# The last graph's final stage in quarters, with three forget products on ScalarE, its stores on SyncE, and a new plan order

## Chip, cores and metric

The kernel runs on one core of a Trainium2 chip. The metric is the device time of one execution in microseconds (us); the median of three runs is compared. A profile of one execution stands beside them: it covers the span from the first to the last instruction, and a little over 3 us of the execution's own time lie outside it.

The engines of a core are named as the profile does: PE is TensorE (matrix products; PEld its weight loads), DVE is VectorE, ACT is ScalarE, POOL is GpSimd, SP is SyncE, which here only issues transfers. Each engine runs its own instructions strictly in order. A transfer is issued by an engine's queue ("SPq", "ACTq") and an instruction that waits holds everything behind it on its engine.

## What is computed

Sixteen graphs of 1024 nodes with 128 features pass through four layers; `adj` is a dense 1024 x 1024 matrix per graph. Each layer adds its result to x. The pieces that matter here are layers 2 and 3.

```python
# layers 0 and 1: three cosine convolutions; then adj aggregation and an MLP
x = x + adapt_conv3(relu(layernorm(x)), adj, ...)
x = x + mlp((1 + eps) * h + h^T adj)            # h = relu(layernorm(x))

# layer 2 (attention)
h = hn @ W                                        # hn = relu(layernorm(x))
attn = softmax(where(adj > 0, tanh(s1[:, None] + s2[None, :]), -1e15))
x = x + where(sum(adj, axis=1) == 0, hn, attn @ h)

# layer 3 (gated attention); x below is relu(layernorm(x))
h = x @ W_w.T + W_b
e = (h @ A) @ h.T;  e = e + e.T
att = softmax(where(adj > 0, e, 0), axis=1) * adj
hp = relu(att @ h)
i, f, o = sigmoid of three linear maps of concat(x, hp)
out = x_in + o * tanh(sigmoid(i * hp + f * x))
```

The last two lines are the final stage: `i`, `f` and `o` are one number per node each (the input, forget and output gates).

## The kernel before

**Tiling.** A graph's 1024 nodes are 8 blocks of 128 (NB = 8); a row buffer `[128, 8*128]` holds all nodes with the nodes of a block on the partitions. Products with the 1024 x 1024 matrices are cut in 8 source blocks and two halves of 512 columns, or, by nodes, in 8 x 8 pieces of 128 columns (`accumulate`, L1543, and `accumulate_nodes`, L1554).

**Order by a plan.** The function `tile_adj_preln` does not emit instructions as it goes. Every step is recorded by `op` (L1071) with its engine, the buffers that it reads and writes and a function that emits it. A step gets a rank: `batch * PERIOD + TIMES[key][nth]`, where the key is made of the layer, the engine and the buffer's name, with own lists for the first two and the last two graphs (" <0", " <1", " >1", " >0"). `Plan.order()` (L136) then picks, again and again, the ready step with the lowest rank whose new buffers fit into the limits of KINDS (L332: how many buffers of a kind there may be in all, and for graphs behind the oldest). The list that results is emitted in that one order, so it fixes the order on every engine and every queue. Steps of up to two later graphs (AHEAD = 2) are mixed in between.

**Layer 2 of a graph** (`layer2`, L1781): `psP` (PE), copies to h (ACT L1813), the products p1 (PE L1867) for s1, then for each of 8 source blocks tanh (ACT L1878), exp (ACT L1882), times the adjacency (DVE L1886), and the sum acc2 (PE L1554). At the end `rden`, `o`, `alone` and x (DVE L1899 to L1907, L1295).

**Layer normalization** (`layernorm`, L1311): statistics on DVE (L1321 to L1332), the power on POOL (L1173), then the scaling half on DVE (L1349), half on ACT (L1356).

**Layer 3** (`layer3`, L1913): sq (PE L1422, and L1439 which adds transposed pieces copied by ACT L1480), a mask of adj (DVE L1956), the masked e and its peak (DVE L1978 and L1987), exp (ACT L1998), times adj (DVE L2007 in two halves; in graph 14, for the odd blocks, POOL L2003), the reciprocal of the sum (DVE L2012), hs (ACT L2016), the sum acc3 (PE L1543); then hpT (ACT L1273), its transposition psN (PE L1251) and the copy hp (ACT L2057).

**The final stage** is the inner function `finish(lo, hi)` (from L2066), for the blocks lo to hi:

1. gate = three columns of hp plus three of h (DVE L2084), tanh (ACT L2108), times 0.5 plus 0.5 (DVE L2109): the three gates.
2. z = hn * forget gate: per block on DVE (L2114) for the last graph, one step on POOL (L2120) otherwise.
3. z = hp * input gate + z: per block on DVE (L2102), or two steps on POOL (L2095, L2096) for graph 14.
4. two tanh on ACT (L2088, L2089): the sigmoid, and the tanh of it.
5. z = z * output gate + x: as step 3.
6. the store of z, issued on ACT's queue (L2127).

For the last graph `finish` runs twice, for blocks 0 to 3 and 4 to 7 (HALVES); for the others once for all eight.

On SyncE's queue, in a middle graph, stand the loads of adj (L1588, and L1630, four issues for each of 8 blocks of adjT), x (L1571), and the store and reload of the transposed pieces (by_hbm L1524, got L1534; near_hbm L1502, back L1512), among others.

Of the kernel before, what the change touches and what calls it, by code (L numbers as in the profile page):

```python
# [12 lines left out]
ALU = mybir.AluOpType  # L13
# [201 lines left out]
def tile_adj_preln(  # L215
# [40 lines left out]
    FLAGS = set("CabcdkxhyzTGmrHWMD3nA")  # L256
# [62 lines left out]
    for load_it in first:  # L319
# [13 lines left out]
        "adjT": ("big", 16, 16), "adjL": ("big", 13, 5), "x": ("big", 5, 3), "w4": ("big", 23, 33),  # L333
        "chunk": ("big", 11, 11), "near": ("near", 2, 1), "quart": ("big", 6, 6), "back": ("big", 7, 1),
        "got": ("got", 1, 1), "ps": ("bank", 8, 8), "acc": ("bank", 7, 4), "small": ("small", 28, 22),
        "row": ("row", 4, 5), "hbm": ("hbm", 2, 3), "hrow": ("hrow", 2, 2), "mask": ("mask", 5, 5),
        "dot": ("dot", 7, 7),
# [4 lines left out]
        "T DMA raw <0": [-13.9, -43.4, -13.95, -48.95, -53.5, -67.75, 2.25, -52.65],  # L342
        "T PE raw <0": [-11.75, -9.15, -8.55, -9.1, -8.85, -11.75, -15.15, -5.25, -12.95, -2.15, 5.8, -17.1,
            -12.75, -12.8, 23.5, 34.25],
        "T ACT adjT <0": [-39.35, -14.15, -18.8, -16.75, -18.35, -7.35, -20.95, -34.55, -13.9, 3.5, 10.4,
            11.05, 16.4, 6.55, -0.6, 4.55],
        "T DVE su <0": [76.75],
        "x DMA x <0": [-13.95, -80.5],
        "0 DVE st <0": [-43.9, -15.15],
        "0 DVE mv <0": [-13.35],  # L350
        "0 POOL rstd <0": [-26.4],
        "0 DVE nb <0": [-22.3],
        "0 DVE hn <0": [-22.25],
        "0 ACT hn <0": [-27.2],
        "0 PE ps <0": [-11.4, -10.65],
        "0 ACT hT <0": [-67.75, -79.6],
        "00 PE psP <0": [-8.6, -54.95],
        "00 DVE h <0": [-22.8, -12.8],
        "00 PE ps <0": [-15, -14.15],
        "00 ACT hTn <0": [-14.35, -18.05],  # L360
        "00 ACT sq <0": [-18.7, -18.25],
        "00 DVE ss <0": [-11.3, -25.55, -15.65],
        "00 POOL rn <0": [-19.1],
        "00 PE sq <0": [-14.45, -7.15, -13.2, -16.05, -11.25, -11.2, -3.15, -2.9, -10.85, 0.7, -11.3, 9.3,
            -12.6, -11.7, 23.5, 14.15, -11.4, -12.7, 28.4, -31.65, 19.7, 36.7],
        "00 ACT near <0": [-18.15, -50.8, -13.85, 12.5, 7.6, 30.05],
        "00 DVE ew <0": [-9.05, -39.7, -6.9, -14.8, -2, 4.75, 8.6, 8.65, 5.75, 2.8, 8.75, -1.6, 7.15, 23.85,
            8.65, 14.9],
        "00 ACT quart <0": [-34.4, -12.1, -34.4, 2.65],
        "00 PE acc0 <0": [-0.8, 4.75, 21.5, 10.9, 1.35, 11.05, 26.05, 32.2, 25.7, 26.55, 27.25, 32.3, 24.45,  # L370
            37.95, 28.35, 29.65],
        "00 POOL params <0": [7.2, 10.25, -5.45, 41.9, 25.85, 20.85, 19.55],
        "00 DMA params <0": [-59.3],
        "00 DVE params <0": [40.65, 44.5, 44.1, 85.55, 81.35],
        "00 PE params <0": [41.95, 46.35, 76.45],
        "00 ACT hT <0": [47.25, 49.1],
        "01 PE psP <0": [-8.35, -10],
        "01 DVE h <0": [48.25, 48.85],
        "01 PE ps <0": [50.4, 52.7],
        "01 ACT hTn <0": [48.4, 52],  # L380
        "01 ACT sq <0": [25.85, 23.6],
        "01 DVE ss <0": [53.65, 33.25, 45.65],
        "01 POOL rn <0": [58.05],
        "01 PE sq <0": [39.9, 53.85, 55, 62.45, 57.8, 58.8, 57.7, 55.5, 49.4, 55.2, 47.35, 62.6, 62, 70.1,
            70.9, 59.9, 70.35, 65.3, 73.9, 62.25, 71.8, 75.4],
        "01 ACT near <0": [40.7, 64.95, 54.05, 64.2, 64.55, 76.4],
        "01 DVE ew <0": [54.65, 71.95, 59.1, 63.15, 60.75, 57.45, 60.35, 72.35, 62, 67.3, 67.6, 74.35, 63.35,
            68.2, 70, 75.65],
        "01 ACT quart <0": [27.55, 57.25, 60, 62.2],
        "01 PE acc0 <0": [63.6, 54.45, 58.6, 75.3, 64.9, 70.85, 62.65, 68.65, 59.35, 55.85, 71.9, 77.45,  # L390
            75.15, 78.85, 55.75, 76.95],
        "01 ACT hT <0": [75.95, 78.9],
        "02 PE psP <0": [56.85, 79.65],
        "02 DVE h <0": [75.4, 75.95],
        "02 PE ps <0": [77.25, 82.75],
        "02 ACT hTn <0": [79.4, 85.7],
        "02 ACT sq <0": [82.15, 71.35],
        "02 DVE ss <0": [76.25, 83.5, 84.75],
        "02 POOL rn <0": [93.55],
        "02 PE sq <0": [88.1, 87.8, 87.1, 91.65, 86.4, 90.15, 90.5, 90.25, 90, 94.25, 93.25, 96.75, 86.65,  # L400
            72.2, 90.25, 102.65, 102.75, 91.2, 103.25, 107.25, 94.75, 105.75],
        "02 ACT near <0": [77.55, 111.75, 89.25, 88.25, 64.25, 97.7],
        "02 DVE ew <0": [87.55, 88.4, 88.7, 84.4, 100.55, 95.75, 101.5, 84.8, 100.9, 106.1, 101.25, 106.65,
            86.6, 98.5, 89.25, 96.95],
        "02 ACT quart <0": [87.7, 88.8, 92.6, 97.3],
        "02 PE acc0 <0": [88.1, 96.95, 93.4, 96.95, 96.8, 99.1, 105.6, 89.8, 105.15, 107.3, 109.7, 110.7,
            106.1, 107.25, 100.3, 112.3],
        "02 DVE x <0": [95.3, 119.3],
        "T DMA adjT <1": [-196.95, -203.05, -216.2, -199.3, -194.4, -213.7, -216.25, -222.2],
        "T DVE adjT <1": [-137.45, -132.6, -132.15, -120.3, -114.25, -114.7, -109.45, -109.25],  # L410
        "T ACT su <1": [-112.25, -101.7, -91.85, -99.6, -96.95, -98.45, -73.5, -89.85],
        "1 DVE st <0": [115.9, 117],
        "1 DVE mv <0": [104.1],
        "1 POOL rstd <0": [113.1],
        "1 DVE nb <0": [120.95],
        "1 DVE hn <0": [113.7],
        "1 ACT hn <0": [134.9, 123.1],
        "1 DVE x <0": [142.15, 140.4, 142],
        "1 DMA adjL <0": [73.65, 69.65, 70.5, 72.6, 137.9, 140.25, 103.9, 109.9],
        "1 DVE adjL <0": [117.85, 77.2, 117.9, 112.65, 124.45, 128.5, 136.25, 134.45],  # L420
        "1 PE acc1 <0": [116.85, 125.15, 129.35, 131.55, 130.25, 139.9, 127.9, 129.3, 129.15, 130.2, 133.75,
            126.35, 132.45, 137.05, 135.2, 135.8],
        "1 ACT g <0": [126.85, 131],
        "1 PE py <0": [137.25, 137.2, 141.6, 137.5],
        "1 ACT y1 <0": [139.75, 138.3, 143.15, 139.8],
        "1 PE py2 <0": [137.75, 128.75],
        "2 DVE st <0": [142.85, 134.25],
        "2 DVE mv <0": [124.2],
        "2 POOL rstd <0": [144.35],
        "2 DVE nb <0": [145.05],  # L430
        "2 DVE hn <0": [147.9],
        "2 ACT hn <0": [129.45, 155.45],
        "2 PE ps <0": [149.7, 146.8],
        "2 ACT hnT <0": [139.55, 69.3],
        "2 DVE alone <0": [138.4],
        "2 DVE x <0": [161.8, 184.9, 184.95],
        "2 PE psP <0": [157.25, 149.45, 149.4],
        "2 ACT h <0": [143.95, 126.95, 127],
        "2 DVE hrow <0": [152.75],
        "2 PE pf <0": [162.6],  # L440
        "2 ACT hfl <0": [164.9],
        "2 PE pt <0": [161.2],
        "2 ACT sr <0": [161.25],
        "2 DMA sd <0": [165.2],
        "2 DMA s1 <0": [163.65],
        "2 DVE h <0": [162.4],
        "2 ACT e2 <0": [144.05, 141.25, 144.1, 150.85, 151.5, 172.6, 151.55, 172.65, 172.65, 172.55, 172.7,
            169.7, 175.8, 179.7, 173.4, 171.75],
        "2 DVE e2 <0": [129.85, 111.65, 158.25, 168.4, 91.05, 87.6, 83.25, 88.25, 170.45, 170.4, 171.75,
            173.1, 164.2, 164.1, 179.1, 179.1],  # L450
        "2 PE acc2 <0": [166.95, 171.9, 153, 177.75, 168.15, 153.4, 178.1, 177.75, 164.45, 167.35, 177.75,
            177.75, 153.2, 172.45, 166.3, 183.1, 171.45, 178.3, 180.65, 182.95, 180.95, 177.55, 175.7, 157.2],
        "2 DVE rden <0": [191.25, 127.75, 127.75, 191.6],
        "3 DVE st <0": [189.2, 171.65],
        "3 DVE mv <0": [191.5],
        "3 POOL rstd <0": [193.55],
        "3 DVE nb <0": [154.25],
        "3 DVE hn <0": [161.35],
        "3 ACT hn <0": [188.7, 253.8],
        "3 PE ps <0": [203.7, 195.9, 200.55, 165.7],  # L460
        "3 ACT hnT <0": [191.15, 186.3],
        "3 PE pg <0": [204.35, 201.8],
        "3 ACT gT <0": [198.15, 200.95],
# [683 lines left out]
    def blk(b, lo, hi, w=D):  # L1147

        return (b, lo * w, hi * w)
# [1099 lines left out]
```

## Time and profile before

| | us |
|---|---|
| median of 3 runs (lowest, highest) | 2362.98 (2362.1, 2363.3) |
| the profiled execution | 2363.82 |
| its span | 2360.7 |
| mean granted TensorE clock | 0.997 of full speed |

| engine | busy us | share of the span |
|---|---|---|
| VectorE | 2069.4 | 88% |
| ScalarE | 1427.9 | 60% |
| GpSimd | 251.6 | 11% |

TensorE's work is the same for every graph, but the first graph starts with nothing to overlap and the last ends with nothing to overlap: the shares above are means over three unlike stretches. How they differ is read from the busy time by windows, from the chain of waits (the work that ended last, followed back from the end) and from the timeline.

The rows of the final stage, in order of time: hp copies of the last graph end at 2348.80; the two gate steps on VectorE start at 2348.50 and 2348.84 (0.17 each), the two gate tanhs at 2348.86 (0.40 together); the forget products at 2349.31 and 2351.23 (four each, 0.88 and 0.87); the products with hp at 2350.18 and 2352.01 (four each, 1.14); the first half's tanh pair at 2351.35, the second's at 2354.71; the last product ends at 2357.26, its store is issued at 2357.35 and the span ends at 2360.7.

Durations that recur below, from the groups of the same page and from the single lines: L1998 exp of 128x1024 1.14 us, L2007 (128x512) 0.67, L1956 (mask, 128x1024) 0.69, L1978 (128x512) 0.68, L2016 (128x128 on ScalarE) 0.40, L1356 (128x128 on ScalarE) four in 1.65.

### The profile page before, as it was taken

Reading aid. Unit: us, or ns where it says so; the run is one execution under the profiler, and the core shown is the slowest. Engines: PE = TensorE matmul, PEld = TensorE weight load, DVE = VectorE, ACT = ScalarE, POOL = GpSimd, SP = SyncE. Lnnn points to the kernel's source line nnn. Section 1 sums busy time; section 2 is a strip of 40 time slices with the busy share of each in tenths; the row PEclk is TensorE's granted clock in tenths of the full one; section 3 lists DMA queues with packets and bytes.
Section 4 is the critical chain, followed back from the end, with each engine's and each line's share of the span. In section 5 each row is a group of like instructions: output and inputs, shape, how many; then the busy total and the mean of one; then the engine's idle time right before and its main releaser. Section 6 shows DMA issues by size and latency. Waiting matters only on the chain.

```text
span 2360.7 us, 35122 instructions
## 1 busy us (share of the span) xinstructions
PE 2327.0 (99%) x11433; PEld 1536.6 (65%) x11433; DVE 2069.4 (88%) x5738; ACT 1427.9 (60%) x2489; POOL 251.6 (11%) x168
## 2 busy tenths in 40 slices
PE   8999999999999999999999999999999999999997
PEld 5568566675756657566675756657566675766763
DVE  6668899999998999999999998999999998887777
ACT  5526764656566565665656667565665656656375
POOL 3001010100101110010100101110010100100022
PEclk9999999999999999999999999999999999999998
DMA  9135759587695867849787695867949677362100
GB/s 189 63 114 117 137 142 187 148 170 146 169 180 150 183 131 182 177 133 190 151 168 154 167 180 148 183 131 183 174 133 192 149 148 134 81 126 63 54 1 18
DMA packets 1048326, 333.17 MB, mean 141 GB/s; under 512 B 721240, under 2 KB 1029600, under 8 KB 1048144
## 3 DMA queue, kind: packets, MB, share of 16 engines
q1 hardware_dynamic: 1027984, 320.24, 62.7%
q10 hardware_dynamic: 19264, 9.70, 1.4%
q8 instruction: 90, 1.47, 0.3%
q0 software_dynamic: 896, 1.01, 0.2%
q14 instruction: 92, 0.75, 0.1%
HBM read 236.94 MB, written 93.91 MB: 140 GB/s over the span
## 4 chain that ended last, share of the span: by engine, by line
PE 92%; DVE 3%; SPq 2%; DMA 1%; ACT 1%; issue 0%; POOL 0%; ACTq 0%; DVEq 0%
PE acc L1543 34%; PE sq L1422 20%; PE acc L1554 19%; PE psP L1251 6%; PE sq L1439 3%; PE py L1774 2%; PE py L1261 2%; SPq L1630 2%; PE ps_hTn L1180 1%; PE pg L1261 1%; PE psN L1251 1%; PE ps_hnT L1180 1%; DVE e L1978 1%; DVE e L2007 1%; PE ps_h3T L1180 1%; SPq L1606 1%
## 5 line engine op out<-in xcount | busy, mean ns | idle before, releaser
L1543 PE MATMUL acc<-ew,h 128*128 128x512 f32 x1024 | 465.9, 593 | 0.5 <-DVE ew L1709 0.5
L1709 DVE SCALAR_TENSOR_TENSOR ew<-sq,rn,adjT 128x512 f32<-128x512 f32 (+3 forms) x612 | 409.0, 703 | 37.9 <-PE sq L1439 13.9
L1422 PE MATMUL sq<-hTn 128*128 128x512 f32 (+3 forms) x1152 | 424.0, 487 | 1.5 <-DVE peak L1978 0.7
L1480 ACT COPY near<-sq 128x384 f32<-128x384 f32 (+2 forms) x312 | 113.6, 369 | 322.9 <-PE sq L1439 275.8
L1543 PEld LDWEIGHTS acc<-ew,h 128*128 128x128 f32 x1024 | 184.9, 190 | 189.1 <-issue 164.8
L1422 PEld LDWEIGHTS sq<-hTn 128*128 128x128 f32 x1152 | 192.3, 191 | 115.8 <-issue 72.6
L1554 PEld LDWEIGHTS acc<-h,ew 128*128 128x128 f32 x2048 | 241.8, 192 | 27.2 <-issue 21.0
L1554 PE MATMUL acc<-h,ew 128*128 128x128 f32 x2048 | 246.7, 275 | 0.0
L1554 PEld LDWEIGHTS acc<-h,e 128*128 128x128 f32 x2048 | 234.8, 192 | 15.2 <-issue 10.5
L1543 PE MATMUL acc<-e,hs 128*128 128x512 f32 x512 | 240.9, 597 | 3.4 <-DVE top L1987 2.0
L1554 PE MATMUL acc<-h,e 128*128 128x129 f32 x2048 | 236.5, 275 | 0.8 <-DVE e L1886 0.6
L1173 POOL TENSOR_TENSOR rstd<-ve,mhalf 128x8 f32<-128x8 f32 x64 | 109.1, 1705 | 1151.8 <-DVE ve L1332 1143.9
L1543 PE MATMUL acc<-adjL,hn 128*128 128x512 f32 x512 | 229.6, 592 | 0.0
L1886 DVE SCALAR_TENSOR_TENSOR e<-adjT,e 128x512 f32<-128x512 f32 x256 | 160.6, 683 | 12.6 <-ACT e L1882 12.4
L2007 DVE TENSOR_TENSOR e<-e,adjT 128x512 f32<-128x512 f32 x248 | 168.6, 701 | 1.3 <-ACT e L1998 1.3
L1998 ACT ACTIVATE e<-e,top 128x1024 f32<-128x1024 f32 x128 | 146.5, 1145 | 33.6 <-DVE top L1987 32.3
L1978 DVE CUSTOM_DVE_ANT_0 e<-mask,sq 128x512 f32<-128x512 int8 x204 | 133.8, 679 | 36.7 <-ACT near L1480 29.7
L1543 PEld LDWEIGHTS acc<-adjL,hn 128*128 128x128 f32 x512 | 94.7, 190 | 107.2 <-issue 103.0
L1543 PEld LDWEIGHTS acc<-e,hs 128*128 128x128 f32 x512 | 93.8, 191 | 106.1 <-issue 93.2
L1638 DVE STREAM_TRANSPOSE adjT<-adjT 128x1024 f32<-128x1024 f32 x120 | 147.8, 1233 | 2.7 <-DMA adjT<-in_adj_dram 2.7
L1422 PE MATMUL sq<-h3T,gT 128*128 128x512 f32 (+3 forms) x384 | 144.2, 488 | 1.8 <-DVE peak L1978 0.8
L1878 ACT ACTIVATE e<-s,h 128x1024 f32<-128x1024 f32 x128 | 142.6, 1137 | 2.8 <-DMA s<-sd 1.7
(169 smaller groups left out, 3675.2 us busy)
## 6 DMA issues: line engine op xcount, KB each, us to landing
adjL<-in_adj_dram SPq DMA_DIRECT2D x128, 512.0 KB
adjT<-in_adj_dram SPq DMA_DIRECT2D x480, 128.0 KB
by_hbm<-quart SPq DMA_DIRECT2D x104, 512.0 KB
got<-by_hbm SPq DMA_DIRECT2D x416, 128.0 KB
near_hbm<-laid SPq DMA_DIRECT2D x24, 384.0 KB
back<-near_hbm SPq DMA_DIRECT2D x96, 96.0 KB
s<-sd SPq DMA_DIRECT2D x15, 512.0 KB
out_dram<-z ACTq DMA_DIRECT2D x15, 512.0 KB
```

Of the source, the lines that this page charges most:

```text
L1251: nc.tensor.matmul(dst.t[:, (c - lo) * n : (c - lo + 1) * n], one(srcT, c), w, start=True, stop=True)
L1422: lambda: nc.tensor.matmul(dst.t[:, (first - lo) * P :], one(leftT, j), some(rightT, first, hi), start=True, stop=True),
L1480: lambda: nc.scalar.copy(span(kept.t, p, p + hi - first), read.t[:, (first - lo) * P :]),
L1543: lambda s=s, lo=lo, hi=hi: nc.tensor.matmul(acc[s].t, cols(h.t, at, w), span(ew.t, lo, hi), start=(j == 0), stop=(j == NB - 1)),
L1554: nc.tensor.matmul(a.t[:, (c - lo) * n : (c - lo + 1) * n], cols(ew.t, c), h.t[:, at * w : at * w + n], start=(j == 0 and c == lo), stop=( ...
L1638: dve(V(N), [t], [t], lambda t=t: nc.vector.transpose(t.t, t.t), True)
L1709: lambda view=view, ew=ew, rn=rn, j=j, lo=lo, hi=hi: nc.vector.scalar_tensor_tensor(like(view(), span(ew.t, lo, hi)), view(), rn.t[:, j : ...
L1878: lambda e=e, j=j: nc.scalar.activation(e.t[:, 0:N], s1.t[:, 0:N], AF.Tanh, bias=h.t[:, j * E2 + D + 1 : j * E2 + D + 2]),
L1886: lambda e=e, j=j, lo=lo, hi=hi: nc.vector.scalar_tensor_tensor(span(e.t, lo, hi), span(aT[j].t, lo, hi), 0.0, span(e.t, lo, hi), op0=ALU. ...
L1978: lambda e=e, view=view, mask=mask, peak=peak, at=at, lo=lo, hi=hi: nc.vector.tensor_tensor_reduce(like(view(), span(e.t, lo, hi)), like(v ...
L1998: lambda e=e, top=top, tot=tot: nc.scalar.activation(e.t[:, 0:N], e.t[:, 0:N], AF.Exp, bias=top.t, accum_out=tot.t),
L2007: lambda e=e, j=j, lo=lo, hi=hi: nc.vector.tensor_mul(span(e.t, lo, hi), span(e.t, lo, hi), span(aT[j].t, lo, hi)),
```

## The change

It has two parts. The first is in the last graph's final stage. `finish` is split into `gates` (step 1, still in halves) and `finish` (steps 2 to 6), which runs over four quarters of two blocks. For the last three quarters, six blocks, the forget product is an activation of the kind Copy on ScalarE, with the gate as its scale; the first quarter's stays on VectorE. The last graph's four stores (two blocks each) are issued by SyncE. A flag "q" turns this on.

```diff
-    FLAGS = set("CabcdkxhyzTGmrHWMD3nA")
+    FLAGS = set("CabcdkxhyzTGmrHWMD3nAq")
...
+    QUARTERS = ((0, 2), (2, 4), (4, 6), (6, 8))
...
-        def finish(lo, hi):
+        def gates(lo, hi):
             n = hi - lo
             at = (gate, 3 * lo, 3 * hi)
...
+        def finish(lo, hi):
+            n = hi - lo
+            at = (gate, 3 * lo, 3 * hi)
...
+                def of_x_by_scalar():
+                    for k in range(lo, hi):
+                        nc.scalar.activation(cols(z.t, k), cols(hn.t, k), AF.Copy, scale=gate.t[:, 3 * k + 1 : 3 * k + 2])
+
-                dve(n * 0.17, [blk(hn, lo, hi), at], [blk(z, lo, hi)], of_x)
+                if "q" in FLAGS and lo >= 2:
+                    act(n * 0.3, [blk(hn, lo, hi), at], [blk(z, lo, hi)], of_x_by_scalar)
+                else:
+                    dve(n * 0.17, [blk(hn, lo, hi), at], [blk(z, lo, hi)], of_x)
...
-                lambda: nc.scalar.dma_start(out[b].rearrange("(c p) d -> p c d", p=P)[:, lo:hi], part(z)),
+                lambda: (nc.sync if final and "q" in FLAGS else nc.scalar).dma_start(
+                    out[b].rearrange("(c p) d -> p c d", p=P)[:, lo:hi], part(z)
+                ),
...
-        for lo, hi in HALVES if "h" in FLAGS and b == B - 1 else ((0, NB),):
-            finish(lo, hi)
+        parts = HALVES if "h" in FLAGS and b == B - 1 else ((0, NB),)
+        for lo, hi in parts:
+            gates(lo, hi)
+        for lo, hi in QUARTERS if "q" in FLAGS and b == B - 1 else parts:
+            finish(lo, hi)
```

The second part is the plan. Every list of TIMES has new numbers (under the same names, with as many entries, and longer lists for the last graph's final stage), and the limits of KINDS differ:

```diff
-        "adjT": ("big", 16, 16), "adjL": ("big", 13, 5), "x": ("big", 5, 3), "w4": ("big", 23, 33),
-        "chunk": ("big", 11, 11), "near": ("near", 2, 1), "quart": ("big", 6, 6), "back": ("big", 7, 1),
-        "got": ("got", 1, 1), "ps": ("bank", 8, 8), "acc": ("bank", 7, 4), "small": ("small", 28, 22),
-        "row": ("row", 4, 5), "hbm": ("hbm", 2, 3), "hrow": ("hrow", 2, 2), "mask": ("mask", 5, 5),
-        "dot": ("dot", 7, 7),
+        "adjT": ("big", 16, 22), "adjL": ("big", 9, 5), "x": ("big", 4, 9), "w4": ("big", 25, 33),
+        "chunk": ("big", 20, 13), "near": ("near", 2, 1), "quart": ("big", 4, 12), "back": ("big", 3, 4),
+        "got": ("got", 1, 1), "ps": ("bank", 7, 8), "acc": ("bank", 6, 4), "small": ("small", 29, 25),
+        "row": ("row", 6, 6), "hbm": ("hbm", 3, 2), "hrow": ("hrow", 1, 1), "mask": ("mask", 5, 5),
+        "dot": ("dot", 12, 8),
```

The sets of instructions of all other stages are the same. In the emitted order most of TensorE's instructions of the middle graphs keep their place (81% stand at the very same position, nearly all others within one microsecond of work); in the first two and last two graphs about a third move. The moves that the prediction speaks of:

- start: the first four transposes `raw_0_0_0` (PE) now follow the first four of hn, instead of leading;
- SyncE, each middle graph: the four issues of the next graph's last adjT block stand ahead of the store by_hbm of its layer 0, instead of behind it;
- graph 15, layer 2: one group of psP, four transposes of graph 14's sq and one small product stand ahead of p1; on VectorE four masked e steps (L1978) of graph 14 stand ahead of the L2007 of its block 0;
- graph 15, layer 3, on VectorE: masks 2 and 3 stand earlier, mask 4 follows the first peak, masks 6 and 7 stand between other e steps, and the gate step of graph 14 (L2109) has three masks ahead of it instead of four; sums and products of blocks 3 to 6 are interleaved differently;
- on ScalarE, graph 14's tanh pair stands ahead of the exps of blocks 2 and 3 of graph 15 instead of behind them; on TensorE more products acc3 of late blocks stand behind the e steps.

## The prediction

> **What bounds the kernel now.** I read the page first: the share of busy time and the chain that ended last, by engine.
>
> ```profile
> PE 2327.0 (99%) x11433; PEld 1536.6 (65%) x11433; DVE 2069.4 (88%) x5738; ACT 1427.9 (60%) x2489; POOL 251.6 (11%) x168
> ...
> PE 92%; DVE 3%; SPq 2%; DMA 1%; ACT 1%; issue 0%; POOL 0%; ACTq 0%; DVEq 0%
> ```
>
> TensorE holds the end for 92% of the span. Next the busy time by stretches (length, then each engine's busy time; the number behind POOL is the granted clock).
>
> ```profile
> 1279.00:1421.00 142.00, 142.00 (x695) 93.68 (x694) 131.52 (x365) 88.52 (x152) 13.86 (x9) 1.00 0.79 165
> ...
> 2200.00:2300.00 100.00, 97.14 (x601) 73.73 (x600) 76.89 (x236) 58.36 (x103) 13.96 (x7) 1.00 0.08 27
> 2300.00:2361.00 61.00, 43.72 (x166) 23.79 (x164) 45.39 (x136) 32.01 (x64) 14.25 (x7) 0.89 0.05 18
> ```
>
> A middle graph leaves PE no hole in 142 us: with the same matmuls (the change adds and removes none) an order can't make it shorter, only longer. Room lies at the start (the first 60 us hold 50.70 of PE work) and in the last 100 us, so I read the chain of waits there (start, length, what), in two windows.
>
> ```profile
> 2299.57 1.74 DVE alone L1906
> ...
> 2317.72 2.11 DVE mask L1956
> ```
>
> ```profile
> 2330.97 2.32 DVE mask L1956
> ...
> 2333.89 2.15 DVE e L2007
> ...
> 2336.85 9.66 PE acc L1543 x18
> ```
>
> Four VectorE steps stand out: a mask takes 0.69 us elsewhere, L2007 0.67, L1906 works on 8 columns. What they share is the timeline of GpSimd:
>
> ```profile
> 2296.05 5.22 POOL L2003 TENSOR_TENSOR e<-e,adjT 128x1024 f32<-128x1024 f32 x2 [16.82 <-ACT e L1998]
> ...
> 2330.35 2.39 POOL L2095 TENSOR_TENSOR z<-z,gate 128x1024 f32<-128x1024 f32 x1 [8.48 <-ACT z L2089]
> 2332.82 2.67 POOL L2096 TENSOR_TENSOR z<-z,x 128x1024 f32<-128x1024 f32 x1
> ```
>
> Each lies under one of these POOL products and ends just after it: while POOL works, such a VectorE step is held, while L1978 runs at its usual 0.68. Last, two of TensorE's waits from 2200 us on (two more, of 2.0 us for a top at 2336.85 and 1.3 for an hs at 2330.55, stand in the same view), and the timeline of the final stage.
>
> ```profile
> PE p L1867 <- ACT h L1813: 1.3, 1, 1.3
> PE sq L1422 <- DVE peak L1978: 0.8, 1, 0.8
> ```
>
> ```profile
> 2354.28 0.38 ACTq L2127 DMA_DIRECT2D out_dram<-z  x1
> 2354.71 0.63 ACT L2088 ACTIVATE z<-z 128x512 f32<-128x512 f32 x1 [1.98 <-DVE z L2102]
> 2355.37 0.72 ACT L2089 ACTIVATE z<-z,half 128x512 f32<-128x512 f32 x1
> 2356.12 1.14 DVE L2102 SCALAR_TENSOR_TENSOR z<-z,gate,x 128x128 f32<-128x128 f32 x4 [1.93 <-ACT z L2089]
> ```
>
> The second half's input was ready at 2353.15 (L2102, 2352.01 + 1.14), but its tanh stood on ACT behind the first store, which waits for VectorE: 1.56 us lost.
>
> **The final stage.** Hp copies end at 2348.80 in either kernel. Both gate tanhs end at 2349.26 (2348.86 + 0.40), so the L2109 steps of 0.17 are done at 2349.28 and about 2349.45. ScalarE then does six new forget products in a row; nearest row hn L1356, four in 1.65, so 0.41 each: 2349.30 + 2.48 = 2351.78. Then four tanh pairs of 256 columns, not in this trace. A pair takes 1.38 at 512 (2351.35 to 2352.73) and 2.23 at 1024 (2327.98 to 2330.21); half of the 0.85 between them less gives 0.95 (an estimate), and 0.1 overlaps between pairs: 3.5, to 2355.28. VectorE closes with two L2102 of 0.285 and a hop of 0.06, at 2355.9 against 2357.26: 1.3 us. VectorE's share (two products 0.44, eight L2102 2.28) is done by 2352.2 and hides under ScalarE. Four handovers instead of two; I take 1.1. From the other side: pairs that don't shrink below 1.38 (5.2 for four) and products at the 0.47 maximum of L2016 (2.8) end at 2357.9, 0.6 later than before. The stores leave ScalarE for SyncE, idle by then: the 0.38 in front of a tanh goes (in the sum above). The last store takes 2.97 us from its issue's end to the span's end; with half the bytes it could lose up to half, 1.5; I take none. Bounds: -0.6 to 2.8.
>
> A rule speaks against the moved product: the Trainium skill's "ScalarE: Activation LUTs", section "Rules for kernel authors", sends multiplications to VectorE. Rows agree on the price (0.22 in L2114, 0.41 here): with all eight products on VectorE its 24 steps are 1.76 + 4.56 = 6.3 from 2349.45, to 2355.8, so by the rule the tail would end 0.1 sooner without the move, and by the rows as well: the gain comes from the quarters and the queue.
>
> **Order, 2265 to 2300 us.** The wait for L1813 (1.3 us) gets four transposes and a small matmul moved in front, about 0.45. The wait for peak (0.8 us) came behind an L2007 held for 1.82; in the new order VectorE runs four L1978 there first, so it goes: 1.25 in all, if acc2 of graph 15 ends as much earlier. Then comes L1906, at 2299.49 on its row. If it arrives over 0.85 us earlier it is in time for the end of the first POOL product (2296.05 + 2.6 = 2298.65) and the gain is 2.5; if less, it waits for 2301.27 all the same, and it is 0. I take 1.25, bounds 0 to 2.5.
>
> **Order, 2312 to 2346 us.** VectorE's chain ends here, TensorE follows. Three holds cost 1.50 + 1.71 + 1.55 = 4.76 (2.19, 2.40, 2.22 less the usual). In the new order graph 14's gate (L2109) is one mask (0.63) earlier, so POOL starts earlier and the first hold shrinks by as much; two masks stand further forward; graph 14's tanh pair goes ahead of two exps (2 x 1.14), so POOL's last two products come some 3 us earlier. There, by the new order, they meet one L2007 and one mask again: I count 1.6 and 1.0 instead of 3.26. Saved: 0.6 + 0.65, less 0.2 of a third mask at the end of a POOL product: about 1.0. Removing the waits of 2.0 and 1.3 gives no more by itself: acc3 can't end before the last L2007 (2343.8) and four passes of 0.43; it ends 2.5 us after it, so 0.8 could go. Bounds: -0.5 (one more hold of 0.5) to 1.9.
>
> The 2.0 wait carries more than itself: behind it six matmuls took 4.51 us against 2.74 for six at 2332.06, in a stretch of clock 0.89. The Trainium skill's "TensorE: Matmul & The Clock Gate", Part 1, wants some 3.4 us of idleness for that; the row shows it after 2.0. By the page this 1.8 us isn't the wait's price; my sum holds neither, as VectorE ends the stretch.
>
> **Start and middle.** The first raw transposes (four, 1.09 at 7.54) move behind those of hn at 9.62; the wait they filled is empty and they cost up to 0.9 later, or nothing where PE waits again (15.19, 0.24). The stretches from 60 to 570 us leave 4.3 us idle; an order could lose or win some. I take 0, bounds -1.0 to 1.0. Middle: 0.
>
> **Sum.** 1.1 + 1.25 + 1.0 = 3.35. The profiled execution took 2363.82 (span 2360.7 and 3.1 outside): 2360.5. The median of the runs is 0.84 lower: 2359.6.
>
> **Rivals.** (A) The order pays at its upper ends: L1906 slips between the POOL products (2.5), the last chain gives 1.9, the tail 1.3: 5.7, so 2357.3. For: 1.25 is over the 0.85 needed. Against: ScalarE feeds acc2 and POOL alike, and POOL's pair may move with it. (B) Hidden: new holds and PE waits replace the old, L1906 waits for 2301.27, ScalarE binds the tail; only some 0.6 is left: 2362.4. For: POOL has the same 9 products under VectorE. (C) Slower: a wait that repeats. On SyncE's queue the four issues of the next graph's adjT_7 now stand ahead of the store by_hbm of layer 0 (issue at 1411.45, then four adjT in 4.75, then got at 1417.22). The store then issues near 1416.2; a store is read back 2.4 to 2.7 us after its issue (L1840 to L1843, L1502 to L1512), so got comes about 2.5 later. Its first reader is L1709 at 1426.8; 9.6 less 2.7 for the landing leaves 6.9 of cover. Beyond it every 0.1 us costs 1.3 in 13 graphs; it eats the gain from 0.25 a graph, and 0.7 gives 2368.7. Against: 4 us of cover are left, and VectorE has 10 idle us in the graph.
>
> **How the numbers follow.** Forecast 0.42, A 0.37, B 0.12, C 0.09. A change under 0.2% (4.7 us, about what a measurement of this kernel tells from none) counts as the same: faster means under 2358.25, which is A with 0.02 of the forecast's low end: 0.39. Slower means over 2367.7, which only C reaches: 0.09. The same: 0.52. The range takes in A and B to their own spreads, 2355.5 to 2363.6, and leaves out C and A's extreme.
>
> **What would show it.** Tail: ScalarE without a hole from 2349 on, the last L2102 1.1 us sooner after the hp copies; wrong if a 256-column tanh is near 0.6. L1906's length: 0.2 for A, 1 to 2 otherwise. Waits at L1867 under 0.9, at L1422 none. Holds on L1956 and L2007 in the last 45 us adding to some 3.7. A middle graph with less than 141.9 of PE work in 142 would show C.

## The result, and the profile after

The changed kernel's median is 2354.1 us (six runs, 2353.27 to 2354.99); the kernel before, run beside it on the same chip, had 2362.66 (six runs, 2362.1 to 2363.46). The ratio is 0.9964, with a 95% interval of 0.9951 to 0.9977: 8.6 us or 0.36% faster, beyond the 0.2% that counts as a change. The prediction was 2359.6 with a range of 2355.5 to 2363.6: the direction of the sum was right, its size less than half, and the time lies 1.4 us below the range. In line numbers the changed body is 2 to about 14 lines further down: L1251 is now L1253, L1867 is L1869, L1978 is L1980, L2007 is L2009; of the final stage L2102 is L2113, L2088 and L2089 are L2099 and L2100, and the forget products on ScalarE are L2125.

The page of the changed kernel, busy time and the chain that ended last:

```profile
PE 2323.5 (99%) x11433; PEld 1535.2 (65%) x11433; DVE 2063.6 (88%) x5732; ACT 1430.8 (61%) x2499; POOL 252.0 (11%) x168
...
PE 95%; DVE 3%; ACT 1%; DMA 0%; issue 0%; POOL 0%; SPq 0%; DVEq 0%; ACTq 0%
```

TensorE's share of the chain rises from 92% to 95%: less of the end is spent waiting for something else. The profiled run took 2353.27 with a span of 2351.5.

Busy time by stretches, first of the kernel before, in the stretches that the prediction didn't show (length; then busy time and count of PE, PEld, DVE, ACT, POOL; clock, DMA share, GB/s):

```profile
60.00:144.00 84.00, 83.54 (x415) 55.07 (x415) 53.76 (x129) 35.03 (x64) 5.15 (x4) 1.00 0.30 95
144.00:286.00 142.00, 139.68 (x689) 92.07 (x688) 113.92 (x347) 83.93 (x146) 11.21 (x7) 1.00 0.53 110
286.00:428.00 142.00, 141.30 (x679) 91.73 (x678) 130.30 (x351) 82.72 (x148) 13.32 (x8) 1.00 0.74 167
428.00:570.00 142.00, 141.17 (x696) 93.37 (x696) 130.19 (x358) 87.40 (x151) 14.02 (x9) 1.00 0.73 160
```

The same and later stretches of the changed kernel:

```profile
60.00:144.00 84.00, 84.00 (x417) 55.43 (x416) 53.64 (x129) 33.87 (x62) 6.57 (x4) 1.00 0.30 92
144.00:286.00 142.00, 140.59 (x700) 93.21 (x699) 114.98 (x353) 86.17 (x152) 11.42 (x7) 1.00 0.55 113
286.00:428.00 142.00, 141.30 (x677) 91.69 (x676) 130.12 (x349) 82.97 (x148) 11.78 (x8) 1.00 0.74 166
428.00:570.00 142.00, 141.98 (x691) 93.20 (x690) 132.29 (x368) 88.09 (x151) 15.58 (x9) 1.00 0.73 161
1279.00:1421.00 142.00, 142.00 (x693) 93.62 (x692) 131.41 (x367) 88.85 (x152) 13.73 (x8) 1.00 0.78 163
```

From 60 to 570 us TensorE stood idle for 0.46 + 2.32 + 0.70 + 0.83 = 4.3 us before and 0 + 1.41 + 0.70 + 0.02 = 2.1 us after. The middle graph is full in both. So TensorE lost 2.2 us less in this part of the start, where the prediction had put 0. What it waited for there, before and after (in total, times, longest; four smaller rows of before, 1.1 us together, are left out):

```profile
PE psP L1251 <- ACT hT L1273: 1.4, 2, 0.7
PE sq L1422 <- DVE peak L1978: 0.7, 1, 0.7
PE pt L1836 <- ACT h L1813: 0.6, 1, 0.6
PE acc L1543 <- DVE ew L1709: 0.5, 1, 0.5
...
```

```profile
PE psP L1253 <- ACT hT L1275: 0.7, 1, 0.7
PE sq L1424 <- DVE peak L1980: 0.7, 1, 0.7
PE pg L1263 <- ACT hnT L1275: 0.2, 1, 0.2
PE sq L1424 <- ACT h3T L1275: 0.2, 1, 0.2
```

The timelines of TensorE show how two of the waits went, 1.3 us of the 2.2. Before, at 182.56:

```profile
180.04 1.95 PE L1251 MATMUL psP<-w2e,hnT 128*128 128x130 f32 x16
182.56 0.28 PE L1836 MATMUL pt<-ident,h 128*8 128x128 f32 x1 [0.58 <-ACT h L1813]
182.68 1.04 PE L1180 MATMUL ps_hTn<-ident,h 128*128 128x128 f32 x8
```

and after:

```profile
178.57 1.95 PE L1253 MATMUL psP<-w2e,hnT 128*128 128x130 f32 x16
180.36 0.60 PE L1182 MATMUL ps_hTn<-ident,h 128*128 128x128 f32 x4
181.10 0.28 PE L1838 MATMUL pt<-ident,h 128*8 128x128 f32 x1
181.21 0.60 PE L1182 MATMUL ps_hTn<-ident,h 128*128 128x128 f32 x4
```

Four of the eight transposes that stood behind `pt` now stand ahead of it: a filler of the kind that the prediction did see in graph 15, in front of p1 (L1867), which waits for the same copy L1813. One of the two waits of `psP` for hT ends differently. The timeline of VectorE and ScalarE before:

```profile
443.87 1.12 DVE L1295 SCALAR_TENSOR_TENSOR h<-psP,rn,b 128x128 f32<-128x128 f32 x4
444.90 2.18 DVE L2102 SCALAR_TENSOR_TENSOR z<-z,gate,x 128x128 f32<-128x128 f32 x8
...
447.16 0.39 ACTq L2127 DMA_DIRECT2D out_dram<-z  x1
447.60 0.60 ACT L1273 ACTIVATE hT<-acc 128x512 f32<-128x512 f32 x1 [1.21 <-PE psP L1251]
```

and after:

```profile
441.09 2.18 DVE L2113 SCALAR_TENSOR_TENSOR z<-z,gate,x 128x128 f32<-128x128 f32 x8
443.19 1.12 DVE L1297 SCALAR_TENSOR_TENSOR h<-psP,rn,b 128x128 f32<-128x128 f32 x4
...
443.34 0.39 ACTq L2141 DMA_DIRECT2D out_dram<-z  x1
443.78 0.60 ACT L1275 ACTIVATE hT<-acc 128x512 f32<-128x512 f32 x1 [0.17 <-PE ps_hnT L1182]
```

On ScalarE the store of an earlier graph's z stands ahead of hT's copy, and its issue can't go before VectorE has made z. Before, VectorE did four steps of h first, the store was issued at 447.16 and the copy, though the profile names TensorE as what it waited for, began right behind the issue. Now z comes first: ScalarE stands idle for 0.17 us before the copy instead of 1.21, and TensorE, which had waited 0.70 for it at 448.25, doesn't wait.

For the whole span I use one bookkeeping below, worked out from the starts of TensorE's matmuls in each trace: from one start to the next, whatever is more than the matmul's usual pace (0.429 us for a pass of 512 columns, 0.111 for 128, 0.109 for a transpose) is time lost. The work is the same in all kernels, so differences of the span are differences of lost time.

| stretch | lost before | lost after | predicted gain | found |
|---|---|---|---|---|
| 0 to 100 us | 14.1 | 12.6 | 0 | 0 to 1.5 |
| 100 to 450 | 8.41 | 6.41 | 0 | 2.0 |
| 450 to 2245 | 5.44 | 5.17 | 0 | 0.3 |
| 2245 to 2300 | 4.45 | 3.08 | 1.25 | 1.4 |
| 2300 to the transposition psN | 9.29 | 7.84 | 1.0 | 1.45 |
| psN to the end of the span | 12.63 | 9.93 | 1.1 | 2.7 |

The rows from 100 us on sum to 7.8 us. The traces of the runs below that share a part of the order or of the code repeat these rows: from 100 to 450 us 8.4 to 8.7 with the old order and 6.4 to 7.1 with the new, psN to the end 12.5 to 12.7 and 9.9 to 10.0. The 0.3 of the long middle is little beside what traces of the new order alone differ by (5.1 to 5.5). The first row doesn't repeat: five traces of kernels that begin like the one before lost 13.0 to 14.1 us there, eight that begin like the one after 12.6 to 14.3. Of the medians' 8.6 some 0.8 is left for it and for the time outside the span (medians 1.93 and 1.79; the 3.1 of the first profiled run was high for this kernel).

One row needs a correction, as it compares with a single profile of before. There the clock granted to TensorE fell to half for 3.4 us, behind a wait of 2.04 (line of the stretches, 2337.0 to 2340.4 us, clock third from the end):

```profile
2337.00:2340.40 3.40, 3.40 (x5) 1.34 (x6) 3.37 (x11) 2.58 (x5) 0.00 (x0) 0.50 0.00 0
```

Three of the kernels below have the old order there too: tail_only (the new final stage alone), head_splice (only the start new, spliced) and head_order (only the start new, by due times). Their traces show a wait of the same length (2.00 to 2.07), but no such fall. In tail_only the clock is 1.00 in the same stretch, and TensorE has time to wait for VectorE once more:

```profile
2337.10 4.07 PE L1456 MATMUL acc<-e,hs 128*128 128x512 f32 x8 [2.07 <-DVE top L1900]
2341.83 4.53 PE L1456 MATMUL acc<-e,hs 128*128 128x512 f32 x10 [0.66 <-DVE e L1920]
```

These three traces lose about 8.9 us from 2300 to psN, not 9.29. Some 0.4 of the 1.45 found there is this fall of the clock in one run and not the order; what the order gave is 1.05 to 1.1.

### The profile page after: what moved, and what is told of

It is laid out like the page before. It is cut to its first block, busy times and chain, and to the rows that moved or that the text cites. A ratio compares the mean times of both kernels' runs of the same rounds, so it can differ in the third digit from the quotient of the medians.

```text
span 2351.5 us, 35168 instructions
## 1 busy us (share of the span) xinstructions
PE 2323.5 (99%) x11433; PEld 1535.2 (65%) x11433; DVE 2063.6 (88%) x5732; ACT 1430.8 (61%) x2499; POOL 252.0 (11%) x168
## 4 chain that ended last, share of the span: by engine, by line
PE 95%; DVE 3%; ACT 1%; DMA 0%; issue 0%; POOL 0%; SPq 0%; DVEq 0%; ACTq 0%
PE acc L1545 36%; PE sq L1424 20%; PE acc L1556 19%; PE psP L1253 6%; PE sq L1441 4%; PE py L1776 2%; PE py L1263 2%; PE ps_hTn L1182 1%; PE pg L1263 1%; PE psN L1253 1%; PE ps_hnT L1182 1%; DVE e L2009 1%; PE ps_h3T L1182 1%; DVE e L1980 1%; DVE e L1888 0%; PE raw L1182 0%
## 5 line engine op out<-in xcount | busy, mean ns | idle before, releaser
L1711 DVE SCALAR_TENSOR_TENSOR ew<-sq,rn,adjT 128x512 f32<-128x512 f32 (+2 forms) x612 | 410.4, 704 | 36.3 <-PE sq L1441 12.7
L1482 ACT COPY near<-sq 128x256 f32<-128x256 f32 (+2 forms) x312 | 113.7, 369 | 331.0 <-PE sq L1441 295.5
L1980 DVE CUSTOM_DVE_ANT_0 e<-mask,sq 128x512 f32<-128x512 int8 x204 | 134.7, 679 | 41.9 <-ACT near L1482 25.2
L2009 DVE TENSOR_TENSOR e<-e,adjT 128x512 f32<-128x512 f32 x248 | 170.2, 701 | 0.5 <-ACT e L2000 0.5
L1456 DVE STREAM_TRANSPOSE quart<-sq 128x512 f32<-128x512 f32 x208 | 142.4, 698 | 4.8 <-PE sq L1424 4.7
```

Source lines behind the costliest of these rows:

```text
L1456: lambda: nc.vector.transpose(kept.t.rearrange("p (h r q i) -> p r h q i", r=2, q=QUARTER, i=SQ)[:, j % 2], read.t.rearrange("p (q h i) -> ...
L1482: lambda: nc.scalar.copy(span(kept.t, p, p + hi - first), read.t[:, (first - lo) * P :]),
L1711: lambda view=view, ew=ew, rn=rn, j=j, lo=lo, hi=hi: nc.vector.scalar_tensor_tensor(like(view(), span(ew.t, lo, hi)), view(), rn.t[:, j : ...
L1980: lambda e=e, view=view, mask=mask, peak=peak, at=at, lo=lo, hi=hi: nc.vector.tensor_tensor_reduce(like(view(), span(e.t, lo, hi)), like(v ...
L2009: lambda e=e, j=j, lo=lo, hi=hi: nc.vector.tensor_mul(span(e.t, lo, hi), span(e.t, lo, hi), span(aT[j].t, lo, hi)),
```

## The experiments

Four kernels first part the final stage from the order. The medians of the kernel before that they shared are 2362.46 (the first four), 2362.36 (the next four) and 2362.16 (the last four).

**The final stage alone.** The order stays that of before; of the plan only the three lists that place the four quarters' steps are new.

```diff
-    FLAGS = set("CabcdkxhyzTGmrHWMD3nA")
+    FLAGS = set("CabcdkxhyzTGmrHWMD3nAq")
```

> The order of before everywhere; only the last graph's final stage is new (quarters, six forget products on ScalarE, stores on SyncE). Theory 1, from the two traces: the stretch from the last psN matmul to the end is 2.65 us shorter and another 1.35 us outside the span go with the stores' new queue, so 4.0 us below before, about 2358.7. Rival (the prediction's own tail): 1.1 us below, about 2361.5. Both: the first psN of graph 15 starts where it does in before, near 2346.3.

Measured: 2360.5 us (11 runs), ratio 0.9991 [0.9982, 0.9999], -2.0 us; in its trace 10.03 us are lost from psN on, against 12.63: -2.6. The median lies between the two expectations. The gain inside the span is over twice what was predicted for this stage; what I hoped for outside the span isn't there (1.98 us outside, as before). The timeline of the changed kernel says where it comes from:

```profile
2342.76 1.86 ACT L2125 ACTIVATE z<-hn,gate 128x128 f32<-128x128 f32 x6
2342.82 0.48 DVE L2121 TENSOR_SCALAR z<-hn,gate 128x128 f32<-128x128 f32 x2
2343.21 2.19 DVE L2113 SCALAR_TENSOR_TENSOR z<-hp,gate,z 128x128 f32<-128x128 f32 x8
...
2347.07 0.40 ACT L2099 ACTIVATE z<-z 128x256 f32<-128x256 f32 x1
2347.50 0.51 ACT L2100 ACTIVATE z<-z,half 128x256 f32<-128x256 f32 x1
2348.04 0.61 DVE L2113 SCALAR_TENSOR_TENSOR z<-z,gate,x 128x128 f32<-128x128 f32 x2 [0.23 <-ACT z L2100]
```

Hp's copies end at 2342.25, the last product at 2348.65: 6.40 us, against 8.46 before and 7.10 in the prediction. The six products on ScalarE take 1.86 us, 0.31 each, where the row L1356 had made me write 0.41; the tanh pairs follow each other every 0.85 us, as estimated. From the last product to the end of the span 2.85 us pass instead of 3.48.

**The order alone.** New TIMES and KINDS, the final stage of before (the diff above reversed in the changed kernel).

> The new order everywhere, the old final stage (halves, all forget products on VectorE, two stores on ScalarE's queue). Theory 1: the order gives 3.5 us in the first 450 us and 2.8 to 3.1 in the last 100, so 6.5 below before, about 2356.2, and 3.1 us lie outside the span as in before. Rival (the prediction's terms for the order): 2.25 below, 2360.4. If tail_only and order_only add up to the whole change (8.6), the two parts don't interact.

Measured: 2357.36 (11 runs), 0.9978 [0.9969, 0.9987], -5.1 us. So the order is the larger part, with more than its predicted 2.25. Its trace has the start of the changed kernel (6.53 lost from 100 to 450 us) and the tail of the old one (12.63).

**Halves of the plan, by due times.** Two kernels take the lists for the first two graphs (names in "<0", "<1") or for the last two (">1", ">0") from the new plan, and the rest from the old.

One list of the first as an example (the changed kernel's numbers, shifted by a constant):

```diff
-        "T PE raw <0": [-11.75, -9.15, -8.55, -9.1, -8.85, -11.75, -15.15, -5.25, -12.95, -2.15, 5.8, -17.1,
-            -12.75, -12.8, 23.5, 34.25],
+        "T PE raw <0": [-12.7, -5.6, -8.45, -9.05, -2.1, -11.75, -15.2, -5.25, -12.25, -5.3, 5.35, -15.05, 11.1, -13.5, 9.35, 35.5],
```

> The kernel before with only the due times of the first two graphs changed. Theory 1: TensorE reaches the middle graphs 3.4 us sooner (its idle time in the first 450 us falls from 22.5 to 19) and the whole run is 3.4 us shorter, about 2359.3, since the middle graphs have no hole to take it back. Rival (the prediction took 0 for the start): the gain at the start is eaten by the unchanged order of the graphs behind it, 2362.7 within 1 us.

> The kernel before with only the due times of the last two graphs changed, old final stage. Theory 1: 2.8 to 3.1 us below before, about 2359.7, all of it between 2260 us and the last psN. Rival A of the prediction: L1906 slips between two POOL products and this part alone gives 4.4, 2358.3. Rival B: 0 to 0.6, 2362.3.

Measured: 2371.99 (5 runs), 1.004 [1.0027, 1.0052], and 2363.39 (11 runs), 1.0004 [0.9995, 1.0013]. Neither theory said 9.5 us slower. The chain of TensorE's waits of the first one (head_order, 290 to 570 us) shows that it has an order that neither parent had:

```profile
PE psP L1163 <- ACT hT L1185: 7.2, 2, 3.7
```

`psP` waits twice, up to 3.7 us, where both parents wait for 0.7. Behind each of the two waits the granted clock is 0.50 for 3.4 us (from 308.9 and from 455.7), which by itself costs some 1.7 us of TensorE's work each time (an estimate: half of the stretch); with the 5.8 us by which the two waits are longer that makes 9.2 of the 9.5. A due time is only a priority: the planner picks the earliest ready step, and a step of the new lists meets neighbours of the old. The two runs say nothing about the parts of the change; they are a failed design of mine, and the reason for the next three.

**Halves of the order, spliced.** The emitted order itself is cut at a point up to which both kernels have emitted the same set of steps; one order stands ahead of the cut, the other behind it. All three have the old final stage.

```diff
+    PLACES = [...]
+    for o, place in zip(plan.ops, PLACES):
+        o.rank = (place, o.seq)
     ordered = plan.order()
```

The cut of the first lies behind the last psN of graph 2 (at 568 us), of the second at the MLP of layer 1 of graph 15 (2255 us), of the third at the first sums of its layer 3 (2314 us).

> The new order up to the end of graph 2 (about 570 us), from there the order of before to the letter, old final stage; head_order mixed due times, this one mixes nothing. Theory 1 (the new start is worth some 3 us by itself): about 2359.3, TensorE's idle time between 50 and 450 us 7.4 us instead of 10.1, and nothing of it lost behind 570 us. Rival (as in head_order, a new start doesn't fit the old middle): 2362.5 or above, with new waits behind 570 us.

> The order of before up to about 2245 us, from there the new order to the letter, old final stage. Theory 1: 2.3 to 2.8 us below before, about 2359.9; L1906 held some 0.5 us instead of 1.7, 1.3 us won by 2300, the rest in the last chain. Rival (end_order's result: the new end is worth nothing without the new middle): 2362.5 or above.

> The order of before up to about 2316 us, only the last graph's layer 3 behind its second sq in the new order, old final stage. By the prediction's third term 1.0 us below before, 2361.5; by the trace of after 1.4, 2361.1. Rival: nothing, since POOL's products meet VectorE at another place when the steps ahead of them have not moved: 2362.5 within 0.5.

| kernel | median (11 runs each) | ratio | difference |
|---|---|---|---|
| new up to 568 us | 2360.33 | 0.9991 [0.9982, 1.0] | -2.0 |
| new from 2255 us | 2359.66 | 0.9988 [0.9979, 0.9997] | -2.7 |
| new from 2314 us | 2361.85 | 0.9997 [0.9988, 1.0006] | -0.5 |

By the medians the start is worth 2.0 us, the end 2.7: together the 5.1 of the order, within 0.4. The first interval just reaches no gain. But the order alone and the new end alone also differ by the start, and their medians lie 2.4 apart (-5.1 and -2.7). In the trace of the spliced start TensorE stands idle for 3.1 us from 60 to 570 us, against 4.3 before and 2.1 in the changed kernel: its wait for a peak took 1.3 there instead of 0.7. So the size of the start is known as 1.2 to 2.4, not better. The end's trace loses 10.91 us from 2245 on to psN, as the changed kernel (10.92), and 1.4 of its gain lies ahead of 2300 us. Of the last chain alone some 0.3 to 0.5 remains when what stands ahead of it is old (13.06 us lost from 2245 on, where the two traces with the old order and a full clock, tail_only and head_splice, lose 13.4; the third median's interval reaches to no gain): the rest of it needs the steps ahead as well.

**Is a VectorE step held by GpSimd's product?** The prediction rests on that reading of the timelines. In the changed kernel two holds are left on the last chain. GpSimd's part of the timeline:

```profile
2290.47 5.50 POOL L2005 TENSOR_TENSOR e<-e,adjT 128x1024 f32<-128x1024 f32 x2 [16.99 <-ACT e L2000]
...
2322.40 1.91 POOL L2106 TENSOR_TENSOR z<-z,gate 128x1024 f32<-128x1024 f32 x1 [6.42 <-ACT z L2100]
2324.39 2.67 POOL L2107 TENSOR_TENSOR z<-z,x 128x1024 f32<-128x1024 f32 x1
```

and VectorE's under the last two of these:

```profile
2323.00 1.86 DVE L1958 TENSOR_SCALAR mask<-adjT 128x1024 int8<-128x1024 f32 x1
...
2324.85 3.36 DVE L2009 TENSOR_TENSOR e<-e,adjT 128x512 f32<-128x512 f32 x2
```

The mask (0.69 elsewhere) ends 0.5 us behind the first product, the first of the two L2009 runs until 2327.61 and takes 2.08 us more than usual. The experiment takes GpSimd's two steps away: graph 14's last product and sum go to VectorE, eight more steps of 0.34, behind the last L2009 of graph 15.

```diff
-                if not final and ("P" in FLAGS or ("y" in FLAGS and late)):
+                if not final and not (b == B - 2 and g == 2) and ("P" in FLAGS or ("y" in FLAGS and late)):
```

> The changed kernel, with graph 14's last product and sum taken from GpSimd (two steps, L2106 and L2107) and given to VectorE (eight L2113 of 0.285, 2.3 us) behind the last L2009, where VectorE stands idle for 3.6 us. Theory of the holds: the two that cost VectorE 1.17 and 2.08 us in the last chain go, and up to 3.2 us with them, as far as TensorE's own work lets it (4.5 us of its waits lie there): 2351.0 to 2352.0. Rival (the last chain is bound by TensorE or ScalarE and the holds are covered): 2354.1 or, with the 2.3 us in front of the gates, later.

Measured: 2352.06 (5 runs), 0.9955 [0.9943, 0.9968], 2.0 us below the changed kernel's 2354.1 (1.7 to 1.9 if each is taken against the kernel before that ran beside it), though VectorE has more to do. The same two VectorE steps in its timeline (the mask is L1870 here, the product L1921):

```profile
2324.67 0.68 DVE L1870 TENSOR_SCALAR mask<-adjT 128x1024 int8<-128x1024 f32 x1
...
2325.34 1.27 DVE L1921 TENSOR_TENSOR e<-e,adjT 128x512 f32<-128x512 f32 x2
```

Both are back at their usual length. VectorE's last L1921 ends 30.17 us after the first product psP of this layer instead of 33.45: 3.3 us, which is the two holds (1.17 + 2.08). TensorE's lost time falls by 2.66, from 10.92 to 8.26, since acc3 then ends 2.3 us behind that step instead of 1.7. The reading holds.

**The stage's pieces.** Three more kernels, and the changed one again beside them. The stores on ScalarE's queue, all behind its last tanh:

```diff
-                lambda: (nc.sync if final and "q" in FLAGS else nc.scalar).dma_start(
+                lambda: nc.scalar.dma_start(
```

> The changed kernel with the last graph's four stores on ScalarE's queue again; by the order they stand behind the last tanh, so they delay no tanh. Theory: only the issue counts: the first three (0.4 each) can start when the last tanh ends at 2348.0, the fourth some 0.5 later than on SyncE: 0.4 to 0.6 above after_again. Rival (the queue itself or the transfer's landing is what SyncE saves): 1.3 or more above.

All eight forget products on VectorE:

```diff
-                if "q" in FLAGS and lo >= 2:
+                if False:
```

> The changed kernel with all eight forget products on VectorE, quarters and SyncE's stores kept. Prediction's view: VectorE needs 1.76 + 4.56 = 6.3 us from the gates on and the tail ends 0.1 sooner than with the products on ScalarE as the prediction sized them (0.41 each). Theory after the trace (ScalarE needed only 1.86 for six, 0.31 each): 6.3 from 2342.82 ends at 2349.1 against 2348.65, so 0.4 to 0.5 above after_again. In either case the move is worth under 0.6 of the tail's gain.

And graph 14's steps on VectorE as above, with only the last two quarters' forget products on ScalarE:

```diff
-                if "q" in FLAGS and lo >= 2:
+                if "q" in FLAGS and lo >= 4:
```

> z14_dve (graph 14's last steps on VectorE) and only two quarters' products on ScalarE, the second quarter's on VectorE. ScalarE's part of the tail is two products (0.62) shorter and VectorE still has room: 0.5 below z14_dve, about 2.5 below after_again, 2351.5. Rival (VectorE's final products now queue behind the earlier ones): no better than z14_dve, 2.0 below after_again.

> The changed kernel once more, beside the next three on the same chip. If the three parts (final stage 2.0, start 2.0, end 2.7 by the medians so far) simply add, it lies 6.7 below before; if the whole is worth more than its parts, at the 8.3 to 8.6 measured first, about 2354.0.

| kernel | median (runs) | ratio to before | lost from psN on |
|---|---|---|---|
| the changed kernel again | 2353.73 (5) | 0.9964 [0.995, 0.9978] | 9.94 |
| stores on ScalarE | 2354.72 (6) | 0.9968 [0.9956, 0.9979] | 10.34 |
| products on VectorE | 2354.64 (6) | 0.9968 [0.9956, 0.9981] | 9.98 |
| graph 14 on VectorE, two quarters | 2351.38 (5) | 0.9955 [0.9942, 0.9968] | 9.57 |

With the stores on ScalarE the issues come one behind the other (issue rows of the timeline, first of this kernel, then of the changed one):

```profile
2348.00 1.98 ACTq L2141 DMA_DIRECT2D out_dram<-z  x4
```

```profile
2346.18 2.91 SPq L2141 DMA_DIRECT2D out_dram<-z  x4
```

On SyncE the first issue starts with its quarter, and the last one ends at 2349.09, 0.44 us after the last product (2348.65); on ScalarE the four end at 2349.98, 0.83 after it (2349.15). That is the 0.4 us by which the tail is longer. From the end of the last issue to the end of the span 2.4 us pass in both, with 128 KB to store; before, with 256 KB on ScalarE's queue, 3.0. So the 0.6 us that the last store gained go with its size, on either queue; SyncE's queue spares the 0.4 that four issues behind one another would have cost. The medians lie 1.0 apart, with runs that overlap (2354.05 to 2355.29 against 2353.61 to 2355.37); that is between the two expectations, and the trace shows the lower one.

With the products on VectorE the tail is as long as in the changed kernel: 6.41 us from hp to the last product (2343.71 to 2350.12) against 6.40. The medians lie 0.9 apart with runs that overlap (2354.18 to 2355.39 against 2353.61 to 2355.37); I expected 0.4 to 0.5 and the trace shows none of it, so what remains between the medians is not from this stage. Moving the three quarters' products earns nothing; four blocks of the eight on ScalarE are better balanced than either (6.00 us from hp to the last product, against 6.40 in the kernel above with six). That kernel, with both edits, is the fastest that I ran: 2351.38, 2.35 below the changed kernel beside it.

## Why the prediction was wrong

**The step that failed: "Start and middle ... I take 0, bounds -1.0 to 1.0".** The middle is 0 (142.00 of 142 us in both kernels). The start gave 2.0 us from 100 us on in the trace of the changed kernel (4.3 us of idleness from 60 to 570 us become 2.1); its splice gave 2.0 by the median and 1.2 in its trace. The profile before had all that was needed: the view of waits lists nine waits for 4.3 us between 60 and 570 us, and the two orders say what stands ahead of each. I walked through that comparison for the last 100 us alone, and gave the start a symmetrical bound, as if an order could only shuffle its waits. A move of the kind that I priced at 0.45 us in graph 15 stood in graph 1 too, and the swap that freed hT needs one look at what is queued behind a store.

**The final stage, 1.1, was mis-sized: 2.7.** Its mechanism was right: ScalarE runs without a hole, a tanh of 256 columns takes 0.40 (below the 0.6 that would have spoken against it), VectorE hides. Three sizes were off. Six products took 1.86, not 2.48 (0.6 us). The 0.2 that I took off for four handovers isn't there: each quarter's closing steps start 0.03 us after its tanh. And the last store, taken at 0 of up to 1.5, gave 0.6, with half the bytes. I had each bound (up to 2.8) and chose near the low end every time.

**The rule that I weighed.** The Trainium skill's "ScalarE: Activation LUTs", section "Rules for kernel authors", sends multiplications to VectorE; I concluded that the gain comes from the quarters and the queue, not from the move. The run with all products on VectorE agrees: 6.41 us against 6.40. The run with four on ScalarE (0.40 us less than with six) fits that balance decides, not the price of one product (0.22 and 0.31); other splits were not run.

**Order, 2265 to 2300 us: 1.25 predicted, 1.4 found.** In the chain of waits from 2190 us on of the changed kernel (in total, times, longest) both waits that I named, at L1867 and for a peak, are gone; the quart's is new:

```profile
PE sq L1441 <- ACT near L1482: 1.8, 2, 1.3
PE acc L1545 <- DVE e L2009: 1.8, 2, 1.1
PE acc L1556 <- DVE e L1888: 1.2, 2, 0.9
PE sq L1441 <- ACT quart L1482: 0.8, 1, 0.8
```

The step `alone` (L1906, now L1908) did neither of what I offered. GpSimd's pair came 5.6 us earlier with it (2290.47 against 2296.05, of which some 3.7 is the whole kernel being earlier), so the step didn't slip between the two products; it was held to the end of the second (2295.97), but for 0.51 us instead of 1.69. (The "held for 1.82" of the prediction is the part of that L2007 that lies on the chain; the step took 2.77, 2.10 above its usual 0.67. The wait behind it went as foretold.)

**Order, 2312 to 2346 us: 1.0 predicted, 1.05 to 1.1 found, for another reason.** The holds sum to 0.91 + 1.17 + 2.08 = 4.16, not to 3.7, and VectorE's last L2009 comes only 0.3 us earlier in its layer (33.45 us after the first psP against 33.73). But TensorE's second sum is copied 1.68 us behind that step instead of 2.25 (2.65 in the profile with the fall of the clock): 0.6 of the 0.8 that I had noted as "could go" went, and 0.2 lies in transposes of hn. So the size came out by luck, from a term that I had put at 0. I also left out the 1.8 us behind the 2.0 wait, "as VectorE ends the stretch". In that profile it doesn't: TensorE runs without a hole from 2336.85 until its sums are done, and ends 0.4 us later than in the traces with the same order and a full clock. With the full clock VectorE ends it, as I said.

**Rivals.** A (2357.3) had the right direction, with the wrong place: its 2.5 for `alone` didn't come. B (2362.4, nearly all hidden) fell. C needed a middle graph with less than 141.9 us of PE work; it has 142.00, so the cover of 4 us held. The range left out the case that happened, several terms at their upper ends together with the start; all the upper bounds (2.8, 2.5, 1.9 and 1.0) together make 8.2, still less than the 8.6 measured.

**What stays open.** The parts measured by themselves (2.0 start, 2.7 end, 2.0 final stage) sum to 6.7, the whole to 8.4 and 8.6. The traces' own sum from 100 us on is 7.8, or 7.4 without the fall of the clock. The rest may lie in the first 100 us and between runs, where traces of one and the same order differ by more than 1 us.

## What to carry to other kernels

Where a new order is compared with an old one, walk through every wait of the bottleneck engine that the profile lists, in the ramp as well as in the drain: in these kernels, whose middle is full, a wait that got work in front did not come back later. Put GpSimd's large products where VectorE has no short steps that it would hold, or give them to VectorE behind its last urgent step: eight steps of 0.34 us there cost nothing, the two holds that they replaced cost 3.3. To test a part of an order, splice the emitted order; half of a table of due times is a third order.

## What the runs showed of the hardware

- VectorE's products and masks (L2009, L1958) and even a step of 128x8 (L1908, 0.12 usually, 0.63 here) didn't end before GpSimd's running product was over, while L1980, which reads one operand from a sum in PSUM (where TensorE writes), started at 2313.86 under a GpSimd step of 2.51 us and took its usual 0.67. The Trainium skill's "SBUF — State Buffer", section "Who interferes with whom", says that the later of the two fully blocks until the first is finished; the ends agree (`alone` at 2296.01, GpSimd's product at 2295.97).
- Activations of the kind Copy with the scale from a column, 128x128, took 0.31 us each back to back (six in 1.86), where those of hn (L1356) took 0.41 (four in 1.65).
- The last store of 128 KB ended the span 2.85 us behind the product that it waits for, on a free queue; on a queue with three issues ahead of it, 3.27; one of 256 KB on a free queue 3.48. From the end of the issue it was 2.4, 2.4 and 3.0.
- Behind one and the same wait of 2.0 to 2.1 us the granted TensorE clock fell to 0.50 for 3.4 us in one trace (before) and stayed at 1.00 in three others with the same order there (tail_only, head_splice, head_order): a single profile can hold a loss that doesn't belong to the order.
